# One 128x128 weight load for two heads, and slot tests as signs on ACT, in an adjacency attention with experts

## The chip, the cores and the metric

The kernel runs on one core of a Trainium2 chip. The metric is the device time of one execution in microseconds (us): the median of the timed executions.

A core has five engines that run side by side and wait for each other by semaphores. In the profile they are PE (matrix products; PEld is its loading of weights), DVE (vector), ACT (scalar, activations), POOL (GpSimd, here mostly gathers by index) and SP (it issues transfers). A product on PE has a stationary operand, the weights, which is loaded into the array, and a moving operand, whose columns stream past it. `nc.tensor.matmul(out, weights, moving)` is written in that order; the result lands in PSUM, the accumulators' memory, and ACT or DVE fetch it from there.

## The reference, cut to what matters

A layer has two parts: attention among the neighbours in a graph, then a mixture of experts with two of eight chosen for each row.

```python
# x (4096, 512), adj (4096, 4096) of zeros and ones; 8 heads of 64
h = layernorm(x)
q, k, v = (einsum('nd,hdk->hnk', h, W) for W in (Wqs, Wks, Wvs))
scores = einsum('hqk,hmk->hqm', q, k) * 64 ** -0.5
scores = scores + 0.01 * eye - 1e16 * (1 - maximum(adj, eye))
att = softmax(scores, axis=-1)
x = x + einsum('hqm,hmk,hko->qo', att, v, Wo)
# x = x + experts(layernorm(x)): routing by top 2, two layers per expert with gelu
```

The first nodes have many neighbours and the last few; all have few out of 4096.

## The kernel before: the parts that the change touches

The program has three stages.

**Stage one** projects queries, keys and values for all rows and writes them to device memory. Beside that it reads the adjacency and makes, for each tile `i` of 128 queries, a list of the keys that any of its queries has as a neighbour, so that attention skips the rest. A list is filled in chunks of 128 places. The keys are sorted by whether only the first 64 queries, only the last 64, or both need them, so that the first and last chunks of a list serve 64 queries alone (a "half" chunk). The lengths are fixed ahead:

```python
LISTED = [28, 20, 18, 16, ...]        # chunks of each of the 32 tiles; 363 in all
FIRST_ALONE = [10, 6, 5, 5, ...]      # chunks before this one: first 64 queries alone
SECOND_FROM = [25, 14, 12, 10, ...]   # chunks from this one on: last 64 queries alone

def half_of(i, c):                    # c < 0 is the tile's own 128 keys, for all queries
    if c < 0: return None
    a, b = halves[i]
    return 0 if c < a else 1 if c >= b else None
```

To turn counts into places, stage one asks of every slot of a list whether each row's run has begun, by comparing slot numbers with the run's first place. The answers (0 or 1) are weights of a product that picks the row's data by differences of neighbouring rows:

```python
def ranges(i):
    a, b = halves[i]
    return [(0, b), (a, b), (a, listed[i])]

def begun(i):
    for k, (t0, t1) in enumerate(ranges(i)):
        ...
        nc.gpsimd.tensor_scalar(          # on POOL
            started[i, k], slots[:, t0 * P : t1 * P], base[g][:, k, j : j + 1], None,
            op0=ALU.is_ge)

def list_rows(i, k):                      # one chunk t of a list
    of = [(0, 0)] if h == 0 else [(2, 3)] if h == 1 else [(0, 0), (1, 1), (2, 2)]
    for n, (q, r) in enumerate(of):
        nc.tensor.matmul(pr[:, t, :], started[i, q][:, s], row_x[g][:, r, j, :], ...)
```

POOL also gathers mask rows ahead (`pm`), which are packed into device memory, and DVE finds which keys have a flag (`neighbours`, one reduction of a 128x4096 tile for each of the 32 tiles).

**Stage two**, attention, goes through 395 items: for each tile its own keys (c = -1) and then its listed chunks. An item's keys and values come by a gather. In step n PE turns the keys of item n+3, makes the scores of item n+2 and uses the values of item n. P is 128, KD 64, NP 4 (pairs of heads), QH 64.

```python
def turn(n):                              # keys: [key, head x 64] to [head x 64, key]
    pk = ps_k.tile([P, 2, TB], F32, ...)
    for p in range(NP):
        for r in range(2):
            half = slice(r * KD, (r + 1) * KD)
            nc.tensor.transpose(pk[:, r, ts(p, KD)], kv[n][half, ts(p, P)], ident[half, half])
    nc.scalar.copy(kT[n].rearrange(...), pk[...])

def scores(n):
    s = [ps_s.tile([P, NP, P], F32, ...) for r in range(2)]
    for p in range(NP):
        for r in range(2):
            rows = slice(r * KD, (r + 1) * KD)          # one head: 64 rows of the array
            nc.tensor.matmul(part(s[r], i, c)[:, p, :], k[rows, p, :], q_in[i][rows, p, q], ...)
    for r in range(2):
        nc.scalar.activation(e[:, r * NP : (r + 1) * NP], part(s[r], i, c), AF.Exp)

def values(n):
    for p in range(NP):
        for r in range(2):
            h = 2 * p + r                               # one head: 64 columns of the array
            nc.tensor.matmul(
                po[i][r * KD : (r + 1) * KD, p, q], v[:, ts(h, KD)], e[:, r * NP + p, :], ...)
    if c >= 0:
        nc.vector.tensor_add(acc[i][:, :, q], acc[i][:, :, q], e)
```

`masked(n)` (DVE) multiplies e by the mask. At the end of a tile the sums of e (`sums`), their inverses (`rb`, a product with 128x128 weights and 128 moving columns), the output product (`py`, 128x128 weights and 512 moving columns) and the routing's transposes (`pt_b`, 128x128) follow, spread over the next items.

**Stage three** runs the experts over sorted blocks of 128 rows.

Of the kernel before, what the change touches and what calls it, by code (L numbers as in the profile page):

```python
# [43 lines left out]
def kernel(  # L44
# [174 lines left out]
    def load_q(i):  # L219
        q_in[i] = qp.tile([P, NP, P], F32, tag="q", name=f"q_{i}")  # L220
        nc.sync.dma_start(out=q_in[i], in_=qT_d[:, :, ts(i, P)])
# [46 lines left out]
    with tc.tile_pool(name="wqkv", bufs=1) as wp, tc.tile_pool(name="p1", bufs=3) as work, tc.tile_pool(  # L268
# [39 lines left out]
        )  # L308

# [21 lines left out]
        def list_constants():  # L331
# [4 lines left out]
            nc.vector.memset(again_c[:, :, :, 0:1], 0.0)  # L336
            nc.vector.tensor_scalar_mul(corner, corner, -1.0)
# [62 lines left out]
        def count_3(g):  # L400
# [24 lines left out]
            base[g] = b  # L425

        def steps(g):

# [3 lines left out]
            nc.tensor.matmul(  # L432
                pd[:, 1:], corner, x_g[:, :2], start=False, stop=True, skip_group_check=True
            )
            pe = ps_l.tile([P, G, NX], F32, tag="l", name=f"pe_{g}")
            nc.tensor.matmul(pe, step, x_g[:, 2], start=True, stop=True)
            dx = lp.tile([P, 4, G, NX], BF16, tag="dx", name=f"dx_{g}")
            nc.scalar.copy(dx[:, :3], pd)
            nc.scalar.copy(dx[:, 3], pe)
# [7 lines left out]
        def begun(i):  # L447

            g, j = divmod(i, G)
            for k, (t0, t1) in enumerate(ranges(i)):  # L450
                if t0 == t1:
# [5 lines left out]
                nc.gpsimd.tensor_scalar(  # L457
                    started[i, k], slots[:, t0 * P : t1 * P], base[g][:, k, j : j + 1], None,
                    op0=ALU.is_ge,
# [5 lines left out]
        def list_rows(i, k):  # L465
# [4 lines left out]
            for t in range(m):  # L470
                h = half_of(i, t0 + t)

                of = [(0, 0)] if h == 0 else [(2, 3)] if h == 1 else [(0, 0), (1, 1), (2, 2)]
# [8 lines left out]
        def list_keys(i, k):  # L482
# [21 lines left out]
            for h, u0, u1 in ((0, 0, a), (None, a, b), (1, b, listed[i])):  # L504
                u0, u1 = max(u0, t0), min(u1, t0 + m)
                if u0 < u1:
                    u = slice(at[i] + u0, at[i] + u1)
                    k = key[:, u0 - t0 : u1 - t0]
                    if h is None:
                        nc.vector.tensor_scalar_add(mask_of[:, u], k, float(i * (N + 1)))  # L510
                    else:
                        nc.vector.tensor_scalar(
# [102 lines left out]
        def pack():  # L615
            i, c = ready.pop(0)
            m = work.tile([P, P], F32, tag="mask", bufs=6, name=f"pm_{i}_{c}")
# [6 lines left out]
        for u in range(8 * NTB + 1):  # L624
# [26 lines left out]
            if u - 2 in load_at:  # L651
                neighbours(load_at[u - 2])
                if load_at[u - 2] == NT - 1:
# [4 lines left out]
                    q_cm = tc.tile_pool(name="q", bufs=2, side="right")  # L658
                    qp = q_cm.__enter__()
                    load_q(0)  # L660
# [41 lines left out]
    def route_1(m, l, pool, name):  # L702
# [4 lines left out]
        ahead = pool.tile([P, m, E, E], F32, tag="ahead", name=f"ahead_{name}")  # L707
        nc.vector.tensor_tensor(ahead, other, own, op=ALU.is_gt)
        same = pool.tile([P, m, E, E], F32, tag="same", name=f"same_{name}")
# [133 lines left out]
    with tc.tile_pool(name="p2a", bufs=2) as two, tc.tile_pool(  # L843
# [38 lines left out]
        def load_x(i):  # L882
            x_in[i] = two.tile([P, D], F32, tag="xt", name=f"xr_{i}")
            nc.sync.dma_start(out=x_in[i], in_=x[ts(i, P), :])
# [3 lines left out]

# [16 lines left out]
        def part(t, i, c):  # L905

            if half_of(i, c) is None:
                return t
# [195 lines left out]
        for n, (i, c) in enumerate(items):  # L1104
# [5 lines left out]
            if c == 2:  # L1110
                load_x(i)
# [307 lines left out]
```

## Time and profile before

| what | us |
|---|---|
| timed executions, median of 3 (range) | 2416.37 (2408.73 to 2416.6) |
| the profiled execution, span | 2203.7 |
| stage one, to about | 505 |
| attention, to about | 1610 |
| slot tests on POOL (L457), 96 instructions | 229.0 |
| key transposes on PE (L893), busy | 172.4 |
| scores on PE (L922), busy | 409.4 |
| values on PE (L954), busy | 311.3 |

The profiled execution was 212 us shorter than the timed ones. The busy time of a group of overlapping instructions is the time in which at least one of them ran. The ends of products on PE are modelled; their starts are the better measure, so the distance from start to start says what a group costs. A "granted clock" of 1 is the full TensorE clock.

### The profile page before, as it was taken

How to read it: one execution, taken by the hardware profiler on the slowest of the kernel's cores; microseconds unless marked ns; L12 is line 12 of the kernel's file. 1: busy time of each engine (PE TensorE's matmuls, PEld its weight loads, DVE VectorE, ACT ScalarE, POOL GpSimd, SP SyncE). 2: the span in 40 equal slices, each digit the busy share in tenths (PEclk: the TensorE clock that was granted, in tenths of full speed). 3: DMA queues.
4: the chain of work that ended last, by engine and by line, in shares of the span. 5: the costliest groups of instructions: out<-in, count | busy, mean ns of one | idle time of the engine just before them, and what ended most of it. 6: DMA issues, size and time to landing. Idle time of an engine off the chain costs nothing. (4 is left out here: it accounts for less than half of the span.)

```text
span 2203.7 us, 52479 instructions
## 1 busy us (share of the span) xinstructions
PE 2040.5 (93%) x20620; PEld 1366.7 (62%) x20620; DVE 1319.2 (60%) x2387; ACT 870.1 (39%) x1842; POOL 1242.8 (56%) x1072
## 2 busy tenths in 40 slices
PE   7877879899999999999999999999829999999998
PEld 3333334348888888888788878777614444444444
DVE  4888586724887767777677777777723222333232
ACT  2121211124666646655556555656412222222222
POOL 1769888885888657678676766667412112111112
PEclk9988988896999989999999999999959999999999
DMA  7737787847788868878788878878475556555554
GB/s 281 301 127 234 258 294 261 263 120 236 247 260 273 273 216 275 281 239 282 247 268 266 267 249 248 264 234 252 165 257 127 134 131 136 136 134 140 137 136 96
DMA packets 215039, 481.71 MB, mean 219 GB/s; under 512 B 49618, under 2 KB 81874, under 8 KB 210692
## 3 DMA queue, kind: packets, MB, share of 16 engines
q0 software_dynamic: 79232, 242.18, 37.1%
q1 hardware_dynamic: 134404, 234.01, 33.7%
q8 instruction: 168, 2.75, 0.5%
q10 hardware_dynamic: 1152, 2.10, 0.3%
q14 instruction: 83, 0.68, 0.1%
HBM read 400.59 MB, written 77.58 MB: 217 GB/s over the span
## 5 line engine op out<-in xcount | busy, mean ns | idle before, releaser
L225 POOL DMA_INDIRECT kv<-kv_d,key_of x363 | 430.4, 1186 | 231.8 <-PE po L954 136.4
L941 DVE TENSOR_TENSOR e<-e,mask 128x512 f32<-128x512 f32 (+1 forms) x363 | 322.6, 889 | 204.0 <-ACT e L932 200.4
L922 PE MATMUL s<-q,kT 64*128 64x64 f32 (+1 forms) x5808 | 409.4, 282 | 2.7 <-ACT acc L932 2.7
L1354 POOL DMA_INDIRECT out_dram<-y,r x71 | 110.6, 1558 | 474.0 <-ACT h L1324 124.7
L922 PEld LDWEIGHTS s<-q,kT 64*128 64x128 f32 x5808 | 373.4, 196 | 2.9 <-ACT acc L932 2.9
L896 ACT COPY kT<-pk 128x512 f32<-128x512 f32 x395 | 232.1, 588 | 285.1 <-PE pk L893 277.3
L932 ACT ACTIVATE e<-s 128x256 f32<-128x256 f32 (+1 forms) x726 | 297.1, 461 | 101.5 <-PE s L922 98.6
L960 DVE TENSOR_TENSOR acc<-acc,e 128x512 f32<-128x512 f32 (+1 forms) x363 | 320.4, 883 | 1.4 <-PE po L954 1.4
L954 PE MATMUL po<-e,kv 128*64 128x64 f32 (+1 forms) x5808 | 311.3, 251 | 0.0
L225 POOL DMA_INDIRECT mask<-in_adjT_dram,mask_of x230 | 257.7, 1121 | 71.9 <-issue 50.0
L457 POOL TENSOR_SCALAR started<-slots,base 128x384 bf16<-128x384 int16 (+12 forms) x96 | 229.0, 2401 | 76.6 <-DVE longer L407 75.7
L954 PEld LDWEIGHTS po<-e,kv 128*64 128x64 f32 x5808 | 246.4, 141 | 34.7 <-issue 0.8
L1318 PE MATMUL ph<-w,xT 128*128 x568 | 258.3, 598 | 0.7 <-ACT xT L207 0.7
L1347 PE MATMUL py<-w,hT 128*128 x568 | 255.6, 593 | 0.9 <-DVE hT L1332 0.9
L352 DVE TENSOR_REDUCE flags<-adjT 128x64 f32<-128x4096 f32 x32 | 141.2, 4413 | 81.2 <-DMA adjT<-in_adjT_dram 81.2
L1352 DVE TENSOR_TENSOR y<-py,bb 128x512 f32<-128x512 f32 x71 | 49.1, 692 | 225.6 <-PE py L1347 184.2
L893 PE MATMUL pk<-ident,kv 64*128 64x64 f32 x2904 | 172.4, 240 | 11.4 <-ACT kT L896 11.0
L893 PEld LDWEIGHTS pk<-ident,kv 64*128 64x128 f32 x2904 | 122.0, 142 | 77.0 <-issue 47.2
L1318 PEld LDWEIGHTS ph<-w,xT 128*128 128x128 f32 x568 | 103.2, 192 | 104.1 <-issue 103.0
L1347 PEld LDWEIGHTS py<-w,hT 128*128 128x128 f32 x568 | 102.5, 190 | 104.0 <-issue 102.8
L225 POOL DMA_INDIRECT pm<-in_adjT_dram,mask_of x133 | 130.5, 981 | 41.5 <-issue 33.6
L1353 ACT ACTIVATE y<-y,gate 128x512 f32<-128x512 f32 x71 | 51.2, 722 | 213.1 <-DVE y L1352 213.1
(589 smaller groups left out, 2405.3 us busy)
## 6 DMA issues: line engine op xcount, KB each, us to landing
adjT<-in_adjT_dram SPq DMA_DIRECT2D x32, 2048.0 KB
bb<-in_L_ffn_b_dram SPq DMA_DIRECT2D x142, 256.0 KB
r<-xs_d SPq DMA_DIRECT2D x71, 258.0 KB
kv_d<-kv SPq DMA_DIRECT2D x32, 512.0 KB
xt<-in_x_dram SPq DMA_DIRECT2D x32, 256.0 KB
qT_d<-qT SPq DMA_DIRECT2D x8, 1024.0 KB
q<-qT_d SPq DMA_DIRECT2D x32, 256.0 KB
xr<-in_x_dram SPq DMA_DIRECT2D x32, 256.0 KB
```

The source lines that it names most:

```text
L225: nc.gpsimd.indirect_dma_start(out=to, out_offset=None, in_=src, in_offset=bass.IndirectOffsetOnAxis(ap=of[:, at[i] + c : at[i] + c + 1], ...
L352: nc.vector.tensor_reduce(flags[g][:, :, j, :], adj_in.pop(i).rearrange("p c (h q) -> p h c q", h=2), axis=AX.X, op=ALU.max,)
L457: nc.gpsimd.tensor_scalar(started[i, k], slots[:, t0 * P : t1 * P], base[g][:, k, j : j + 1], None, op0=ALU.is_ge,)
L893: nc.tensor.transpose(pk[:, r, ts(p, KD)], kv[n][half, ts(p, P)], ident[half, half])
L896: nc.scalar.copy(kT[n].rearrange("k p (r j) -> k r p j", r=2), pk[:, :, : NP * KD].rearrange("k r (p j) -> k r p j", p=NP),)
L922: nc.tensor.matmul(part(s[r], i, c)[:, p, :], k[rows, p, :], q_in[i][rows, p, q], start=True, stop=True,)
L932: nc.scalar.activation(e[:, r * NP : (r + 1) * NP], part(s[r], i, c), AF.Exp)
L941: nc.vector.tensor_mul(e, e, m.unsqueeze(1).to_broadcast(e.shape))
L954: nc.tensor.matmul(po[i][r * KD : (r + 1) * KD, p, q], v[:, ts(h, KD)], e[:, r * NP + p, :], start=(c < 0 and p == 0), stop=(c == listed[i ...
L960: nc.vector.tensor_add(acc[i][:, :, q], acc[i][:, :, q], e)
L1318: nc.tensor.matmul(ph, xTs[b][:, c, :], w1[:, bass.ds(es[b], 1), c, :], start=(c == 0), stop=(c == DC - 1),)
L1347: nc.tensor.matmul(py, hTs[b][:, c, :], w2[:, bass.ds(es[b], 1), c, :], start=(c == 0), stop=(c == HC - 1),)
```

## The change

**In attention**, the two heads of a pair share one weight load of 128x128. The queries of a pair are laid out block-diagonally (each head's rows in its own half of the columns, zeros elsewhere; the zeros are written once into two fixed tiles), so that one product of 128 rows gives the scores of both heads side by side. For the values, both heads' columns of v are loaded together and both heads' e move past; of the result, the two diagonal blocks are used and the others are not. The aim is half as many products and weight loads. Keys are turned by full 128x128 transposes. The result of a tile takes two PSUM banks, and four copies on ACT (`take`) pick out the used blocks.

**In stage one**, the tests of slots move from POOL to ACT as signs (-1 or 1 in place of 0 or 1). The differences are halved, and a constant is added through one more product so that the sums come out the same. The row numbers of mask rows (`mask_of`) are written by POOL in place of DVE. Some buffers shrink to make room (`ahead`, `same`, `pm`, `xr`, `o`), and x of a tile is loaded later.

The core of the diff; cuts are marked by `...`:

```diff
 def load_q(i):
-    q_in[i] = qp.tile([P, NP, P], F32, tag="q", name=f"q_{i}")
-    nc.sync.dma_start(out=q_in[i], in_=qT_d[:, :, ts(i, P)])
+    q_in[i] = q_two[i % 2]
+    for r in range(2):
+        rows = slice(r * KD, (r + 1) * KD)
+        nc.sync.dma_start(out=q_in[i][rows, :, r, :], in_=qT_d[rows, :, ts(i, P)])
...
+            past_b = lp.tile([P, 3, G], F32, tag="past_b", name=f"past_b_{g}")
+            nc.vector.tensor_scalar(past_b, b, -1.0, 0.5, op0=ALU.mult, op1=ALU.add)
...
-            dx = lp.tile([P, 4, G, NX], BF16, tag="dx", name=f"dx_{g}")
-            nc.scalar.copy(dx[:, :3], pd)
-            nc.scalar.copy(dx[:, 3], pe)
+            dx = lp.tile([P, 5, G, NX], BF16, tag="dx", name=f"dx_{g}")
+            nc.scalar.mul(dx[:, :3], pd, 0.5)
+            nc.scalar.mul(dx[:, 3:], pe, 0.5)
...
-                nc.gpsimd.tensor_scalar(
-                    started[i, k], slots[:, t0 * P : t1 * P], base[g][:, k, j : j + 1], None,
-                    op0=ALU.is_ge,
+                nc.scalar.activation(
+                    started[i, k], slots[:, t0 * P : t1 * P], AF.Sign,
+                    bias=base[g][:, k, j : j + 1],
                 )
...
-                        nc.vector.tensor_scalar_add(mask_of[:, u], k, float(i * (N + 1)))
+                        nc.gpsimd.tensor_scalar_add(mask_of[:, u], k, float(i * (N + 1)))
...
         def turn(n):
-            for p in range(NP):
-                for r in range(2):
-                    ...
+            for p in range(NP):
+                nc.tensor.transpose(pk[:, p, :], kv[n][:, ts(p, P)], ident)
+            nc.scalar.copy(kT[n], pk)
...
         def scores(n):
-                for r in range(2):
-                    rows = slice(r * KD, (r + 1) * KD)
-                    nc.tensor.matmul(
-                        part(s[r], i, c)[:, p, :], k[rows, p, :], q_in[i][rows, p, q], ...)
+                nc.tensor.matmul(
+                    s[-1][:, p - (len(s) - 1) * NP // 2], k[:, p, :], q_in[i][:, p, :, q], ...)
...
         def values(n):
-                for r in range(2):
-                    h = 2 * p + r
-                    nc.tensor.matmul(
-                        po[i][r * KD : (r + 1) * KD, p, q], v[:, ts(h, KD)], e[:, r * NP + p, :], ...)
+                j, t = divmod(p, NP // 2)
+                nc.tensor.matmul(
+                    po[i][j][:, t, :, q], v[:, ts(p, P)], e[:, 2 * p : 2 * p + 2, :], ...)
...
+        def take(i):
+            osb[i] = single.tile([P, NP, P], F32, tag="o", name=f"o_{i}")
+            for j, t in enumerate(po.pop(i)):
+                for r in range(2):
+                    rows = slice(r * KD, (r + 1) * KD)
+                    nc.scalar.copy(osb[i][rows, ts(j, NP // 2), :], t[rows, :, r, :])
```

A half chunk (64 queries) needs one PSUM bank for the scores of all heads, a full one two.

## The prediction, made before the result was known

> **What bounds the kernel now.** I read the page's busy line first, then the busy time by stretch, then the TensorE timeline of the attention stage instruction by instruction, and last the waits of the first stage.
>
> ```profile
> PE 2040.5 (93%) x20620; PEld 1366.7 (62%) x20620; DVE 1319.2 (60%) x2387; ACT 870.1 (39%) x1842; POOL 1242.8 (56%) x1072
> ```
>
> ```profile
> 0.00:530.00 530.00, 437.19 (x1919) 220.58 (x1919) 344.04 (x693) 113.73 (x203) 391.16 (x368) 0.89 0.70 239
> 530.00:1610.00 1080.00, 1049.52 (x17001) 873.68 (x16999) 800.77 (x1311) 624.20 (x1424) 739.07 (x632) 0.97 0.80 253
> 1610.00:2204.00 594.00, 553.82 (x1705) 272.48 (x1704) 174.42 (x385) 132.15 (x215) 112.59 (x73) 0.97 0.59 137
> ```
>
> The columns are PE, PEld, DVE, ACT, POOL, then the granted clock and the DMA. The program has three stages: projections and lists (to about 505), attention (to about 1610), experts. In attention PE is busy 1049.5 of 1080 us, so a PE microsecond there is a microsecond of the end. In the first stage PE has 93 us of holes at a clock of 0.89, and POOL is the next fullest. The change leaves the third stage alone.
>
> How attention spends PE time is in the timeline of PE. Its columns are start and length in us, then line, operation, weights (rows*columns), moving tile and the count of records.
>
> ```profile
> 1019.16 0.46 PE L893 MATMUL pk<-ident,kv 64*128 64x64 f32 x8
> 1019.45 1.06 PE L922 MATMUL s<-q,kT 64*128 64x64 f32 x16
> 1020.44 0.69 PE L954 MATMUL po<-e,kv 128*64 128x64 f32 x16
> 1021.06 0.46 PE L893 MATMUL pk<-ident,kv 64*128 64x64 f32 x8
> 1021.35 1.11 PE L922 MATMUL s<-q,kT 64*128 64x128 f32 x16
> 1022.39 0.69 PE L954 MATMUL po<-e,kv 128*64 128x64 f32 x16
> 1023.01 1.16 PE L992 MATMUL rb<-rinv,spread 128*128 128x128 f32 x8
> 1024.10 0.46 PE L893 MATMUL pk<-ident,kv 64*128 64x64 f32 x8
> ...
> 1027.39 1.09 PE L954 MATMUL po<-e,kv 128*64 128x128 f32 x16
> 1028.41 3.70 PE L1001 MATMUL py<-wo,o 128*128 128x512 f32 x8
> 1032.05 0.46 PE L893 MATMUL pk<-ident,kv 64*128 64x64 f32 x8
> ```
>
> Three things are to be seen. A product of 32-bit numbers leaves two records, a transpose one. The groups follow each other without a hole. And the small products run **two at a time**: 16 score records of 128 moving columns take 1.11 us, while eight records of the same 128 columns at 128x128 (rb) take 1.16 us. The two row halves of the array work side by side for scores and transposes, and the two column halves for values. Start to start, an item costs: transposes 0.29; scores 0.99 (64 queries) or 1.04 (128); values 0.62 or 1.02. Scores hardly notice the number of queries, so they run at the pace of their weight loads; values do notice it.
>
> Two narrower windows give the pace of products that use the whole array:
>
> ```profile
> 1023.33 0.61 PE L992 MATMUL rb<-rinv,spread 128*128 128x128 f32 x4
> ```
>
> ```profile
> 1028.95 2.31 PE L1001 MATMUL py<-wo,o 128*128 128x512 f32 x5
> ```
>
> The records last 275 and 592 ns (medians of these lines), so the steps are (610-275)/3 = 112 ns at 128 columns and (2310-592)/4 = 430 ns at 512. Between them, 256 columns should step by 112 + 318/3 = 218 ns (an estimate).
>
> **What the Trainium skill says.** (1) "TensorE: Matmul & The Clock Gate", Part 3, packing small matmuls: matmuls in different row or column groups of the array run concurrently. The 16 records in 1.11 us against eight in 1.16 agree. (2) The same page, LDWEIGHTS: a load's time follows its columns, not its rows; it estimates 128 columns at 107 ns. Scores step by (1.06-0.27)/7 = 0.113 us a pair (a record lasts 0.27), nearly the same for 64 and 128 queries, which agrees. (3) "TensorEngine Tiling (Array Packing)", Key Properties: changing the tiling mode drains TensorE. rb occupies 1.09 us from its start to the next group's where eight steps of 112 ns are 0.90, so about 0.2 us goes to entering and leaving; that fits. (4) "ScalarE: Activation LUTs", What ACT_TABLE_LOAD costs: an ACTIVATE with a pointer bias takes about 280 ns + 0.833 ns an element. No instruction here has exactly this form; an estimate below uses it.
>
> **The change in attention.** The weights become 128x128. For scores, the queries of a pair of heads lie in a block diagonal with zeros, and twice the columns move; for values, both heads' columns of v meet both heads' e, and half of what is written is never read. The loads are halved, but the work side by side is lost: each pair that moved 64 or 128 columns once, on both halves of the array together, now moves 128 or 256 columns.
>
> - Transposes: 4 records of 128 columns at 0.112 = 0.45 us, from 0.29.
> - Scores, values, 64 queries: 8 x 0.112 = 0.90 each, from 0.99 and 0.62.
> - Scores, values, 128 queries: 8 x 0.218 = 1.74 each, from 1.04 and 1.02.
>
> So a half item goes from 1.90 to 2.25 us (+0.35), a full one from 2.35 to 3.93 (+1.58). The lists hold 363 items; the full ones are the sum of SECOND_FROM minus FIRST_ALONE, 134, plus the 32 own tiles, so 166 full and 229 half. 229 x 0.35 + 166 x 1.58 = 80 + 262 = **+342 us**. Against it, rb, py and the transposes of routing no longer change the mode: four such groups a tile at up to 0.2 us, 32 tiles, about -20. The four copies that take po now (one before) run on ACT while PE turns and scores, so I give them little. PE can't pass this on: it is at 97% already. DVE (800.8 us of 1080), ACT and POOL only get more room. Net in attention: **+320 us**.
>
> **The change in the first stage.** POOL loses the 96 tests:
>
> ```profile
> L457 POOL TENSOR_SCALAR started<-slots,base 128x384 bf16<-128x384 int16 (+12 forms) x96 | 229.0, 2401 | 76.6 <-DVE longer L407 75.7
> ```
>
> ```profile
> PEld L476 <- POOL started L457: 40.7, 23, 4.6
> PE pr L476 <- POOL started L457: 31.9, 20, 3.2
> ```
>
> From the page's groups and the waits (us in total, times, longest): 229 of POOL's 391 us go away. ACT gets them: 80,768 elements in each partition (128 times the sum of the ranges' lengths) x 0.833 ns + 96 x 0.28 = 94 us (estimate), on an engine busy 114 of 530. PE's two rows name the load and the product of one wait, so they aren't added: about 40 us of PE holes. Beyond them, DVE sits in the same stretch up to 2.86 us in an L510 that takes 0.16 when POOL isn't testing, POOL's mask gathers queue behind tests of 6 us, and the loads of the next adjacency tile wait behind those. All that loosens. What stays: PE's own work, about 24 records of 512 columns a tile x 32 x 0.43 = 330 us plus transposes and lists, some 390; and the transfers, 239 GB/s x 530 us = 127 MB, which at 285 GB/s (the first 60 us) need 445. The stage lasts about 505 us, so at most 60 to 100 can come back. The mask rows moved to POOL are some 100 tiny instructions and cost nothing there. I take **-55 us**.
>
> **Sum.** 2204 + 320 - 55 = about 2470 us in a profile like this one. The timed runs before are 2416, 212 us above the profiled execution, for which the profile has no reason. It does show PE at half pace at the start of attention:
>
> ```profile
> 514.82 1.91 PE L922 MATMUL s<-q,kT 64*128 64x64 f32 x16
> 516.66 1.12 PE L954 MATMUL po<-e,kv 128*64 128x64 f32 x16
> ```
>
> The same 16 records take 1.06 and 0.69 us later. If the timed runs have more of such a clock, the added PE work stretches by the same tenth (265 to 290); if full tiles ease the clock, it shrinks. I choose the plain sum, 2416 + 265 = **2680 us**.
>
> **Rivals.** (a) *Loads are the bound, and halving them pays.* For it: scores take the same time at 64 and 128 queries. If that held for all 40 loads of an item (now 20), about 0.9 us an item or 350 us would be won: 2070. Against it: rb, with one full load a record, steps by 112 ns, twice the 56 of a score record; and values follow the moving columns (0.62 to 1.02). (b) *The clock.* If the 212 us are throttled time that packed tiles cause and full ones (half zeros in the queries) don't, all could come back: 2416 + 265 - 212 = 2470. For it: 40 us at half pace in a full stretch. Against it: the rest of attention, equally packed, stands at 0.97 and more. (c) *The first stage gives everything*, 100 us and a better clock at its end: 2630. (d) *New waits*: ACT, now with signs ahead of its PSUM copies and four copies to empty po, holds up PE. Some us a tile: 2730.
>
> **Range and chances.** The attention term is firm within about 50 us, since its paces come from this trace; the first stage within 50; the unexplained 212 us of the timed runs is the widest. Range 2560 to 2770. Even (b) ends above 2% slower; only (a) makes it faster. Faster 0.04, same 0.05, slower 0.91.
>
> **What would show it.** In the profile after: score and value products with weights 128*128, eight records each, stepping about 112 ns at 128 moving columns and 218 at 256, one at a time; a full item near 3.9 us and a half one near 2.25; PE still full in attention, longer by 300 or more; DVE and POOL shares down there. In the first stage: no POOL tests, ACT up by about 95 us, no PE waits on POOL, the first attention item some 55 us earlier. I would be wrong if 256 columns step at much under 200 ns, or if the clock differs widely between the two.

## The result, and the profile after

| | us |
|---|---|
| kernel before, median (range) | 2416.48 (2408.73 to 2420.38) |
| changed kernel, median of 4 (range) | 2494.18 (2492.32 to 2498.93) |
| ratio, with its 95% interval | 1.033 (1.030 to 1.036) |

The change costs 78 us where 265 were predicted. The busy line of the page of the changed kernel (span 2490.6 us) answers to the first line shown of before:

```profile
PE 2327.0 (93%) x12728; PEld 1663.2 (67%) x12728; DVE 1274.0 (51%) x2297; ACT 982.7 (39%) x1805; POOL 1021.0 (41%) x1080
```

PE has 12,728 instructions in place of 20,620, and yet is busy 287 us longer than in the profile of before. By stretch, in the columns PE, PEld, DVE, ACT, POOL, granted clock and DMA:

```profile
0.00:530.00 530.00, 443.88 (x1926) 232.70 (x1927) 305.70 (x619) 211.36 (x314) 199.17 (x388) 0.94 0.74 248
480.00:1900.00 1420.00, 1374.92 (x9399) 1199.79 (x9397) 821.09 (x1350) 661.54 (x1316) 736.90 (x644) 0.99 0.66 197
```

In stage one POOL falls from 391 to 199 us and ACT rises from 114 to 211. In attention PE is still full, at a clock of 0.99. The timeline of PE in attention, changed kernel (start, length, line, weights, moving tile, count of records):

```profile
1018.07 1.06 PE L1022 MATMUL rb<-rinv,spread 128*128 128x128 f32 x8
1018.97 0.60 PE L915 MATMUL pk<-ident,kv 128*128 128x128 f32 x4
1019.40 1.89 PE L935 MATMUL s<-q,kT 128*128 128x256 f32 x8
1021.13 1.05 PE L976 MATMUL po<-e,kv 128*128 128x128 f32 x8
...
1024.37 1.89 PE L976 MATMUL po<-e,kv 128*128 128x256 f32 x8
1026.09 3.60 PE L1031 MATMUL py<-wo,o 128*128 128x512 f32 x8
1029.53 0.60 PE L915 MATMUL pk<-ident,kv 128*128 128x128 f32 x4
```

From start to start, turns take 0.43, scores at 128 queries 1.73 (256 moving columns), values at 128 queries as much (1026.09 - 1024.37), and values at 64 queries (128 columns) 0.89, up to the next group, at 1022.02, which is cut here. A full item comes to 0.43 + 1.73 + 1.73 = 3.89 us, where 3.93 was predicted. So the products cost what they were said to cost, and the time that is missing from the loss has to be looked for in the kernel before.

### The profile page after: what moved, and what is told of

It is laid out like the page before. It is cut to its first block, busy times and chain, and to the rows that moved or that the text cites. A ratio compares the mean times of both kernels' runs of the same rounds, so it can differ in the third digit from the quotient of the medians.

```text
span 2490.6 us, 36652 instructions
## 1 busy us (share of the span) xinstructions
PE 2327.0 (93%) x12728; PEld 1663.2 (67%) x12728; DVE 1274.0 (51%) x2297; ACT 982.7 (39%) x1805; POOL 1021.0 (41%) x1080
## 3 DMA queue, kind: packets, MB, share of 16 engines
q8 instruction: 106, 1.74, 0.3%
## 5 line engine op out<-in xcount | busy, mean ns | idle before, releaser
L228 POOL DMA_INDIRECT kv<-kv_d,key_of x363 | 446.2, 1229 | 551.3 <-PE po L976 376.5
L935 PE MATMUL s<-q,kT 128*128 128x128 f32 (+1 forms) x2904 | 499.6, 315 | 3.8 <-ACT acc L949 3.8
L976 PE MATMUL po<-e,kv 128*128 128x128 f32 (+1 forms) x2904 | 496.5, 314 | 0.7 <-issue 0.7
L976 PEld LDWEIGHTS po<-e,kv 128*128 128x128 f32 x2904 | 430.0, 192 | 30.7 <-issue 1.3
L935 PEld LDWEIGHTS s<-q,kT 128*128 128x128 f32 x2904 | 418.9, 192 | 25.4 <-ACT acc L949 4.1
L949 ACT ACTIVATE e<-s 128x512 f32<-128x512 f32 x497 | 296.3, 599 | 151.1 <-PE s L935 91.7
L228 POOL DMA_INDIRECT mask<-in_adjT_dram,mask_of x230 | 234.0, 1018 | 73.9 <-issue 68.0
L915 PE MATMUL pk<-ident,kv 128*128 128x128 f32 x1452 | 224.4, 277 | 17.7 <-ACT kT L916 11.0
L915 PEld LDWEIGHTS pk<-ident,kv 128*128 128x128 f32 x1452 | 170.6, 142 | 57.3 <-issue 36.1
L207 ACT COPY xT<-pt_e 128x512 f32<-128x512 f32 x71 | 41.5, 585 | 233.3 <-PE pt_e L206 233.3
```

The lines of the kernel that those rows point to most:

```text
L228: nc.gpsimd.indirect_dma_start(out=to, out_offset=None, in_=src, in_offset=bass.IndirectOffsetOnAxis(ap=of[:, at[i] + c : at[i] + c + 1], ...
L915: nc.tensor.transpose(pk[:, p, :], kv[n][:, ts(p, P)], ident)
L935: nc.tensor.matmul(s[-1][:, p - (len(s) - 1) * NP // 2], k[:, p, :], q_in[i][:, p, :, q], start=True, stop=True,)
L949: nc.scalar.activation(e[:, j * m : (j + 1) * m], t.rearrange("p a r q -> p (a r) q"), AF.Exp)
L976: nc.tensor.matmul(po[i][j][:, t, :, q], v[:, ts(p, P)], e[:, 2 * p : 2 * p + 2, :], start=(c < 0 and t == 0), stop=(c == listed[i] - 1), ...
```

## The experiments

Eighteen runs, told by the question. "Before" is always the kernel before on the same chip, timed beside the run; its level differs by chip, so ratios are compared. A **hole** below is an idle stretch of PE over 0.1 us after which comes a product that has no semaphore to wait for, counted between the first scores and the experts. **Half clock** is time in which the trace's clock records give TensorE half its clock; counted are the stretches that lie wholly between the first scores and the last. Those that reach over either end are told of apart. Several texts speak of the "supply theory": PE loses time because it does not get its instructions fast enough where many of them fall into a short time.

### The kernel before, seen again

Nothing is edited.

> The kernel before, unchanged, to see what its usual execution of about 2416 us looks like beside the profile of 2204 us. Clock theory: the extra 212 us are TensorE at a lower granted clock in the attention stage, where products share the array two at a time; then the executions near 2416 us have a mean granted clock of about 0.85 to 0.88, the first stage (to 505 us) and the expert stage (594 us) are as long as in the profile of 2204 us, and attention lasts about 1290 us in place of 1080. Rival, transfers or gathers are slower in the usual execution: the clock stays at 0.95, PE shows waits on DMA or POOL in attention, or all three stages stretch. Rival, a fixed cost outside the profiled span: span and time differ by 200 us.

Measured: 2429.76 us, ratio 1.001 (0.999 to 1.004), and a span of 2427.5, not 2203.7. Attention is where the two executions of the same kernel part. From the first scores to the first transpose of the experts, in this execution and then in the profile that the prediction was read from:

```profile
508.80:1854.90 1346.10, 1218.96 (x17281) 1006.53 (x17280) 823.02 (x1370) 631.62 (x1449) 732.00 (x646) 0.89 0.67 213
```

```profile
501.60:1639.40 1137.80, 1075.24 (x17282) 897.62 (x17280) 819.57 (x1370) 634.41 (x1448) 755.96 (x649) 0.95 0.79 253
```

That is 208 us more, at a clock of 0.89 against 0.95. (The 0.97 of the prediction is of 530 to 1610 and leaves out most of the half clock at both ends.) PE's timeline in this execution:

```profile
588.16 0.92 PE L954 MATMUL po<-e,kv 128*64 128x128 f32 x11
589.38 0.49 PE L954 MATMUL po<-e,kv 128*64 128x128 f32 x5 [0.30 <-issue]
...
592.90 0.38 PE L922 MATMUL s<-q,kT 64*128 64x64 f32 x2
593.91 0.77 PE L922 MATMUL s<-q,kT 64*128 64x64 f32 x9 [0.62 <-issue]
594.91 0.45 PE L922 MATMUL s<-q,kT 64*128 64x64 f32 x4 [0.23 <-issue]
```

Groups of 16 records are broken into pieces with holes between them, and "issue" says that no semaphore was waited for. Right after this, from 597.7, records last 0.42 us where they last 0.27: the clock has been halved. The view of PE's waits between 510 and 1580 us of this execution adds such idle time up (us in total, times, longest; two of its rows):

```profile
PE s L922 <- issue: 13.6, 34, 1.1
PE pk L893 <- issue: 10.9, 28, 1.1
```

The changed kernel has two rows of that kind in the same stretch:

```profile
PE pk L915 <- issue: 4.7, 7, 1.4
PE po L976 <- issue: 2.6, 5, 0.9
```

By the two windows, PE is idle 127 us of the 1346 here (1346.1 - 1219.0), 65 more than the 63 of the first profile (1137.8 - 1075.2). The rest of the 208 us lies in steps that begin at half clock: set against the median step between the same two groups in the first profile, the steps from start to start at full clock come to the same total in both executions (within 1 us), those at half clock to 144 us more. Half clock is 225 us in 28 stretches here, against 44 in 4. Of the 28, 21 begin within 7 us after a hole; the other seven follow 1.4 to 5.1 us of idle time ahead of products that had a semaphore to wait for.

### The two parts alone

The lists alone (the part of the change in stage one; attention as before):

> The stage-one part of the change alone (signs on ACT, mask rows on POOL), attention as before, packed. My step of the first stage: it ends about 55 us earlier, so about 2360 us against 2416, if the clock in attention is as low as in the usual execution before. Clock theory: mean granted clock again about 0.86. If stage one of the change were worth only the 25 to 30 us by which the first attention item starts earlier in the two profiles so far: about 2390. If the stage-one part is what makes the clock high (POOL no longer interferes): about 2180.

Measured: 2379.87 against 2428.48 us, ratio 0.979 (0.975 to 0.983), so 49 us won. The first scores start at 467.2 in place of 508.8.

Attention alone (stage one as before):

> The attention part of the change alone (128x128 weights for two heads), stage one as before. My step of attention: +320 us on the profile of 2204, so a span of about 2520, and the time like the span, because full tiles keep the clock. Clock theory: mean granted clock 0.95 to 0.97, time 2520, ratio to before about 1.043. If the clock in attention did not depend on the packing, the time would be 2416 + 320 = 2736.

Measured: 2561.89 against 2428.48, ratio 1.056 (1.051 to 1.061), so 133 us lost, clock 0.962 against 0.916. That is nearer to the 2520 of a clock that depends on the tiles than to the 2736 of one that does not. The two parts add up: 133 - 49 = 84, and the whole change costs 78. The first scores start at 535.8, 27 us later than before: part of what the attention change costs lies ahead of attention. In the first 480 us of this trace PE waits 60.5 us for the slot tests on POOL, against 32.1 in the kernel before seen again.

The lists with the mask rows left on DVE:

```diff
-                        nc.gpsimd.tensor_scalar_add(mask_of[:, u], k, float(i * (N + 1)))
+                        nc.vector.tensor_scalar_add(mask_of[:, u], k, float(i * (N + 1)))
```

> The signs on ACT alone; the mask rows stay on DVE, attention as before. My prediction gave the mask rows nothing: then 2380 us as with both. If POOL's mask rows hold back its gathers (its profile shows POOL waiting 140 us for DVE's keys in stage one): 10 to 20 us faster than both, about 2365. If DVE's relief was what helped: slower, about 2395.

Measured: 2347.31 against 2399.85, ratio 0.979 (0.975 to 0.983), the same as the lists with them. The signs on ACT do all of it, the mask rows nothing that can be measured.

### Fewer instructions in half items

The lists, and the scores of half items (64 queries) by one 128x128 load; the rest packed in pairs as before:

```diff
+            if full:
                 for p in range(NP):
                     for r in range(2):
                         nc.tensor.matmul(s[r][:, p, :], k[rows, p, :], q_in[i][rows, p, r, :], ...)
+            else:
+                for p in range(NP):
+                    nc.tensor.matmul(s[0][:, p], k[:, p, :], q_in[i][:, p, :, q], ...)
```

> Stage one of the change; in attention only the scores of half items (64 queries) go by one 128x128 load for two heads, 8 records in place of 16; full items, transposes and values stay packed. Supply theory (PE doesn't get its instructions fast enough where items are short: 80 instructions, products and loads, in 1.9 us, against 80 in 2.36 us of a full item): a half item now has 64 instructions in about the same 1.9 us, 33 in a us, as many as a full item, so the holes inside groups and the half-clock stretches at the ends of tiles go away, about 200 us: from the 2380 us of the lists alone to about 2180. Rival (packed tiles cost the clock by themselves): values and full items are packed as before, so about 2380.

Measured: 2338.99 against 2399.85, ratio 0.975 (0.971 to 0.979): hardly more than the lists alone, and near the rival's 2380 (0.98 of the 2428 that it starts from). Yet the clock changed. Beside the run with the signs alone, on the same chip, which differs from this one by the half items' scores (and by where the mask rows are written, worth nothing), the holes stay (74 of 27.1 us, for 90 of 29.1), and half clock falls from 198 us in 28 stretches to 82 in 17. The first 50 us of attention show it best, signs alone and then with half scores:

```profile
451.50:501.50 50.00, 49.54 (x626) 45.14 (x624) 25.29 (x35) 23.04 (x49) 24.13 (x22) 0.62 0.53 163
```

```profile
488.00:538.00 50.00, 46.98 (x727) 40.87 (x726) 34.76 (x39) 29.29 (x53) 34.42 (x26) 0.99 0.63 190
```

PE is busy nearly all the time in both, and the clock is 0.62 in the one and 0.99 in the other. All 20 traces agree. In the seven with packed scores in half items, the stretch of half clock that lies at the first scores is 20 to 55 us long (41.0 in the profile of before, 47.8 in the kernel before seen again); in the 13 with 128x128 scores there it is 3 to 10. So a stretch of half clock lasts longer where the scores of half items are packed. The number of instructions alone does not do it: with the 64 tiny products told of below it is 6.8 us on both chips. What in the packed scores does was not tried.

The same with all transposes at 128x128:

```diff
-                for r in range(2):
-                    nc.tensor.transpose(pk[:, r, ts(p, KD)], kv[n][half, ts(p, P)], ident[half, half])
+                nc.tensor.transpose(pk[:, p, :], kv[n][:, ts(p, P)], ident)
```

> As the run with half scores, and keys turned by four 128x128 transposes in place of eight of half size. A half item has 56 instructions, 27 in a us. Supply theory: no holes at all; the transposes cost 0.15 us more an item, 395 items, less a mode change saved: about 40 us more than the run with half scores, so 2220; if half scores alone leaves some starvation, the two are closer. Rival (packed tiles cost the clock): 2380 + 40.

Measured: 2331.33 against 2399.85, ratio 0.971 (0.967 to 0.974); 48 holes, 41 us of half clock. Both missed the supply theory's number by 100 us or more: I had taken the holes to go at once. They stand where instructions are still dense: 31 of the 48 lie ahead of or inside the packed values of half items, whose 16 products and 16 loads take 0.62 us, 52 a us.

The changed kernel with only the full items packed again (scores and values; all turns at 128x128):

> The changed kernel with full items packed again: half items (64 queries) take their scores and values by one 128x128 load for two heads (40 instructions in 2.25 us, 18 in a us), full items by two tiles at a time as before (72 in about 2.5 us). Supply theory: no holes, half items at 2.25 us where they now take about 3.2 at the ends of tiles, so attention about 110 us shorter than with the lists alone: about 2250 to 2280, the fastest so far. If instead what a packed kernel loses is tied to packed tiles: full items still lose clock, about 2350. If my cost of a half item were all that counts (2.25 against 1.9): 2380 + 80 = 2460.

Measured: 2352.44 against 2412.57, ratio 0.976 (0.973 to 0.980), the number of the rival by which packed full items lose clock. But that is not what happened: the holes are nearly gone (10, and 17 us of half clock), with the full items packed. It is not quicker for another reason. The timeline of PE shows it, in full items of this kernel:

```profile
599.80 0.66 PE L915 MATMUL pk<-ident,kv 128*128 128x128 f32 x4
600.39 1.16 PE L933 MATMUL s<-q,kT 64*128 64x128 f32 x16
601.48 1.09 PE L982 MATMUL po<-e,kv 128*64 128x128 f32 x16
602.50 0.66 PE L915 MATMUL pk<-ident,kv 128*128 128x128 f32 x4
```

A full item takes 602.50 - 599.80 = 2.70 us and not the 2.35 that it took with packed turns: the turns take 0.59 for 0.29, of which 0.14 is the full array (0.43) and the rest comes where the tiling changes to that of the packed scores. 166 x 0.35 is 58 us, most of the miss. So the last of these kernels packs everything of full items, turns too, and half items have scores and turns at 128x128:

```diff
+            if half_of(*items[n]) is not None:
+                for p in range(NP):
+                    nc.tensor.transpose(pk[:, 0, ts(p, P)], kv[n][:, ts(p, P)], ident)
+                nc.scalar.copy(kT[n], pk[:, 0, :].rearrange("k (p j) -> k p j", p=NP))
+                return
```

> The half-scores kernel (lists part of the change, scores of half items by one 128x128 load, everything of full items packed), with the transposes of half items at 128x128 as well and those of the 166 full items left packed in pairs. The supply theory: a half item gives PE 56 instructions instead of 80 in about the same 1.9 to 2.0 us, so the holes are at most those of the kernel with half scores and all turns at 128x128 (ratio 0.9705, half clock 34 us), and 166 full items save 0.2 to 0.3 us of transposes each against it, 33 to 50 us: about 0.953 of before, some 2290 us. The rival, that the packed transposes of full items bring mode changes and holes that cost as much as they save: 0.970 to 0.976, no better than the two kernels it comes from.

Measured: 2222.09 against **2212.12** us, ratio 1.005 (1.003 to 1.007). Neither number was expected, because the kernel before itself took 2212 us on this chip, in all of 12 executions (2203.5 to 2217.3). The trace of this run has not one hole. A half item takes 2.10 us in it (turns 0.49, scores 0.99, values 0.62, from start to start), 0.20 more than before; 229 x 0.20 = 46 us, about what the lists win, and nothing else is given back. On another chip, where before took 2407.73, the same kernel was run again:

> The kernel with the scores and transposes of half items at 128x128 and everything of full items packed, on another chip. Where before takes about 2212: again 1.005. Where it takes 2400 to 2430: the supply theory gives 2290 (0.953), half clock 35 us or less; the rival, that packed transposes of full items bring holes and mode changes of their own, gives 0.970 to 0.976.

Measured: 2336.13, ratio 0.971 (0.967 to 0.974), with 42 holes and 51 us of half clock: the rival's number. Packing the turns of full items again gained nothing over turning everything at 128x128. Of its holes 23 again lie at the packed values of half items.

### Work added to the kernel before

If PE loses time because it gets its instructions too slowly there, work that needs few instructions should cost less than it takes. The kernel before, with zero products added to the accumulators of 197 half items, one of 256 columns:

```diff
+            if half_of(i, c) is not None and c < listed[i] - 1:
+                nc.tensor.matmul(po[i][:, :2, :], zeros, v[:, : 2 * P], start=False, stop=False, ...)
```

> The kernel before, with work added: in 197 half items one more product of zero weights 128x128 and 256 moving columns, added into the values' accumulator (it adds zeros, so the output stays). 4 more instructions in about 0.64 us (two records of 0.218 and a mode change of 0.2): 126 us of PE in all. Supply theory: 84 instructions in 2.55 us are 33 in a us, so the supply keeps up and most of the about 220 us lost at the tile ends comes back: 2429 + 126 - 200 = about 2350, faster with more work. Rivals (packing or the clock by itself, or waits on other engines): 2429 + 126 = 2555 or more.

Measured: 2435.06 against 2399.85, ratio 1.017 (1.013 to 1.021): 35 us for 126 us of work, in between the two expectations; half clock fell to 92 us. Two of 512 columns each:

```diff
+                for _ in range(2):
+                    nc.tensor.matmul(po[i][:, :, :], zeros, v, start=False, stop=False, ...)
```

> The kernel before with more filler: two products of zero weights and 512 moving columns in each of 197 half items, 8 instructions in about 1.92 us (4 records of 0.43 and a mode change of 0.2), 378 us of PE in all; packing untouched. A half item then has 88 instructions in 3.8 us, 23 in a us, fewer than in the run with half scores and 128x128 turns. Supply theory: the bursts of holes (0.75 us apart, some ten instructions in each, nothing waited for) and the half-clock time (about 210 us of attention) nearly vanish, so the quick execution's 2204 us plus 378: about 2580 to 2620. If packed tiles lose the clock by themselves: before plus 378, 2780 to 2810, and the half-clock time stays.

Measured: 2607.55 against 2412.57, ratio 1.081 (1.077 to 1.085): 195 us for 378 us of work, clock 0.964, half clock 38 us, 28 holes (80 in the kernel before seen again). **183 us came back**, the supply theory's number, with all packing as it was. On a second chip:

> The kernel before with two zero products of 512 columns in 197 half items, 378 us of PE work, on another chip. Where before takes about 2212 us there are no holes to absorb them: about 2590 us, the full 378, ratio 1.17. Where it takes 2400 to 2430: again about 2607, ratio 1.08.

Measured: 2595.56 against 2407.73, ratio 1.077 (1.073 to 1.081), 188 us for 378. The 378 themselves were never seen, since the run did not fall on the chip where before takes 2212.

### Small instructions added to the changed kernel

The opposite edit tells the rate of instructions from the packed tiles: the changed kernel, all at 128x128, gets many products with one moving column of zeros in 197 half items, 32 in the first run:

```diff
+                for u in range(32):
+                    nc.tensor.matmul(po[i][u % 2][:, 0, 0, :1], zeros, ones[:, :1], start=False, stop=False, ...)
```

> The changed kernel, all full 128x128 tiles, with 32 tiny products (zero bf16 weights, one moving column, added into the accumulator) in each of 197 half items: 104 instructions in an item in place of 40. No packing anywhere in it. Supply theory: bursts of holes inside groups appear and half-clock time rises from 20 us to 50 or more; time 2494 + 197 x 32 x 0.03 to 0.06 us (190 to 380) plus what the holes cost. If packing is what costs the clock: no holes, clock stays at 0.97, and 2690 to 2870 by the tiny products alone.

Measured: 2694.81 against 2412.57, ratio 1.118 (1.114 to 1.122), 46 holes, but only 34 us of half clock. Undecided: the holes came, the half clock and the time did not. Then 64:

> The changed kernel with 64 tiny 16-bit products (one moving column of zeros) added in each of 197 half items, where 32 were before. A half item then gives PE 168 instructions in about 2.23 + 64 x 0.025 = 3.83 us, 44 a us, as many as the half items of the kernel before (42). Without any loss the 64 cost 197 x 1.6 = 315 us over the changed kernel: about 2800 us. If the rate of instructions alone makes the holes and the half clock, both come back: over 80 holes without a wait in attention, over 100 us of half clock, 2900 us or more. If they belong to the packed tiles, holes stay near those with 32 tiny products (46) and the half clock under 40 us: 2800 to 2850 us.

Measured: 2787.93 against 2212.12, ratio 1.264 (1.260 to 1.267), no hole, half clock 10 us. It fell on the chip where the kernel before takes 2212 us, so it decides nothing alone. On the chip where before takes 2407.73:

> The changed kernel with 64 tiny products in 197 half items, 44 instructions a us there, on another chip. Where before takes about 2212: again 2788. Where it takes 2400 to 2430: if the rate of instructions alone makes the holes, over 80 holes without a wait in attention, over 100 us of half clock and 2900 us or more; if they belong to the packed tiles, fewer than 50 holes, under 40 us of half clock and 2800 to 2850 us.

Measured: **3066.85** us, ratio 1.275 (1.270 to 1.280), 248 holes of 105 us and 338 us of half clock. The same program differs by 279 us between the two chips. The whole stretch of attention, in the first line on the chip where before takes 2212:

```profile
500.00:2200.00 1700.00, 1666.90 (x21769) 1500.62 (x21765) 824.49 (x1344) 664.15 (x1304) 740.22 (x638) 0.99 0.54 165
```

and on the chip where it takes 2408:

```profile
500.00:2490.00 1990.00, 1845.83 (x21878) 1641.52 (x21877) 826.82 (x1347) 664.79 (x1307) 739.88 (x639) 0.91 0.46 142
```

The group of 64 in PE's timeline, on the first chip:

```profile
1118.66 1.74 PE L985 MATMUL po<-ones,zeros 128*128 128x1 bf16 x64
1120.26 0.63 PE L703 MATMUL pt_b<-ident,rows 128*128 128x128 f32 x4
```

and on the second:

```profile
1104.59 1.22 PE L985 MATMUL po<-ones,zeros 128*128 128x1 bf16 x41
1106.33 0.27 PE L985 MATMUL po<-ones,zeros 128*128 128x1 bf16 x5 [0.52 <-issue]
1107.06 0.27 PE L985 MATMUL po<-ones,zeros 128*128 128x1 bf16 x5 [0.46 <-issue]
1107.79 0.28 PE L985 MATMUL po<-ones,zeros 128*128 128x1 bf16 x5 [0.46 <-issue]
1108.54 0.35 PE L985 MATMUL po<-ones,zeros 128*128 128x1 bf16 x8 [0.48 <-issue]
```

On the first, 64 products take 1.60 us, 25 ns each. On the second, 41 go at that pace, and then PE gets five products, with their five weight loads, every 0.73 us, with half a microsecond of nothing between. The next turns run at half clock (1108.76 to 1109.64, 0.88 us from start to start for 0.43). No tile here is packed, so **such holes need no packing: a large number of instructions in a short time is enough for them**, on one chip and not on the other. The 338 us of half clock come in 63 stretches, 61 of which begin within 7 us after a hole, but they are short (5.4 us in the mean, 8.0 in the kernel before).

### The changed kernel on the two kinds of chip

> The changed kernel, unaltered, on another chip. If the 212 us belong to the chip: where the kernel before takes about 2212 us, the changed one takes 2480 to 2500, a ratio of 1.12 to 1.13; where it takes 2400 to 2430, 2490 to 2500 and 1.03. So the changed kernel's time hardly depends on the chip while that of before does. The rival, that a quick chip speeds up everything alike (2212/2416 = 0.915): 2280 us and 1.03 on both.

Measured: 2485.87 against 2407.73, ratio 1.032 (1.027 to 1.037).

> The changed kernel, unaltered, once more, in the hope of the other kind of chip. Where before takes about 2212 us: 2470 to 2500, a ratio of 1.12 to 1.13, if the 212 us belong to chip and instruction rate; 1.03 if a quick chip speeds up everything alike. Where before takes 2400 to 2430: 1.03 as on two chips already.

Measured: 2493.63 against 2419.30, ratio 1.032 (1.026 to 1.037).

> The changed kernel, unaltered, a last time. Where before takes about 2212 us: 2470 to 2500, ratio 1.12 to 1.13 by the theory that the 212 us belong to chip and instruction rate; 1.03 by the rival that a quick chip speeds up everything alike. Where before takes 2400 to 2430: 1.03 again.

Measured: **2461.42 against 2196.97, ratio 1.120** (1.114 to 1.126). This run came to the same chip as the 2212. The time is 9 us under the expected range, the ratio in it. The difference is 264.5 us. Its attention stretch, changed kernel on this chip:

```profile
470.00:1890.00 1420.00, 1374.17 (x9432) 1200.87 (x9430) 828.32 (x1369) 672.54 (x1321) 764.97 (x654) 0.98 0.67 203
```

Attention looks as it does on the other chips (PE 1374 of 1420 us there and here). The changed kernel hardly knows on which chip it runs (2461 to 2494); the kernel before does:

| chip, as numbered by the runs | kernel before, median us | executions |
|---|---|---|
| 1, 8, 2, 13, 0 | 2428, 2400, 2413, 2408, 2419 | 55, all within 2390 to 2443 |
| 11, on two occasions | 2212, 2197 | 19, all within 2186 to 2218 |

One chip of six is of the quick kind. Instructions of a half item (products and loads, both as records) over the time that it takes without loss, and what the traces hold, on the chips other than 11:

| kernel | instructions a us | holes (us) | half clock, us |
|---|---|---|---|
| changed kernel | 40/2.23 = 18 | 3 (1) | 20 |
| half items at 128x128, full ones packed | 18 (full items 72/2.70 = 27) | 10 (4) | 17 |
| half scores and turns at 128x128 | 56/2.10 = 27 | 48 (20) | 41 |
| changed, 32 tiny products | 104/3.03 = 34 | 46 (23) | 34 |
| before | 80/1.90 = 42 | 80 (26) | 225 |
| changed, 64 tiny products | 168/3.83 = 44 | 248 (105) | 338 |

These are means over an item; inside it the packed values ask for 52. On chip 11 neither 44 a us nor the kernel with half items' scores and turns at 128x128 has a hole, and nor has the profile of before that the prediction was read from, if it is of that kind (42).

## Why the prediction was wrong, step by step

**The paces of attention: right.** 0.90 and 1.74 for a group of eight at 128 and 256 columns were predicted, 0.89 and 1.73 measured; a half item 2.25 and a full one 3.93, against 2.21 to 2.23 and 3.89. The mode changes too: rb takes 0.90 from start to start where it took 1.09, and py 3.44 where it took 3.64, 0.2 us each as put.

**Stage one, -55: right, as a part by itself.** The lists alone gave 49, on a chip of the other kind. The signs cost ACT what was estimated (94 us): the changed kernel's group of them, by line, with its busy time and mean, reads

```profile
L475 ACT ACTIVATE started<-slots,past_b 128x384 bf16<-128x384 int16 (+12 forms) x96 | 89.0, 992 | 74.4 <-DVE within L504 27.6 <-DVE past_b L434 27.3 <-DVE hi L424 11.2
```

and PE no longer waits for POOL there. That the mask rows on POOL are worth nothing held as well.

**The sum, +265: right on one kind of chip, in part by luck.** Chip 11 gave +264.5. By the time of the first scores it divides otherwise than the prediction had it, with the profile of before as the start: -20 ahead (501.6 to 481.4) where -55 was put, and +277 after (1138 to 1415) where +320 was put. The two misses have opposite signs and cancel. Ahead, the lists alone brought the first scores 42 us forward, but attention alone moved them 27 back, which the prediction had at nothing. What in it does that (the zeros that POOL writes into the query tiles, the two loads of queries, the smaller buffers and the later load of x are candidates) was not tried. After, the first profile holds 120 us of half clock and 63 of idle PE in its attention, ends included, and the changed kernel on chip 11 holds 54 and 50. That is worth some 33 + 12 us (an estimate: half of the difference in half clock, all of that in idle time), which a sum of paces leaves out and which makes up the 43 between 277 and 320. If the lists win 49 on chip 11 too, which was not run, the attention part as a whole costs about 314 there.

**From the sum to the timed runs, "I choose the plain sum, 2416 + 265": this step failed.** It treated the 212 us by which the timed executions exceeded the profile as a part of the program that the change leaves alone, or stretches by a tenth. They were a loss of the kernel before on five of the six chips: its half items ask for 42 instructions a us, PE is left without for some tenths of a microsecond at a time (65 us more of idle PE), and it runs at half clock more often, for longer where half scores are packed (144 us more). The changed kernel asks for 18, packs neither scores nor values, and loses little: 2490 on those chips where it takes 2461 on chip 11, against 2416 and some 2205 for before. Before loses 211 us there and the changed kernel 29, so 182 came back: 265 - 182 = 83, and 78 were measured.

**The rivals.** (b), "the clock", had the number (2470) and a large part of the cause. That throttled time would come back was right. That packed tiles bring it is right in part: with the holes nearly the same, half clock fell from 198 to 82 us when the scores of half items alone were unpacked. But packing alone does not bring it: with full items packed and half ones not, half clock is 17 us, and tiny products at full tiles bring holes and half clock too. What I held against it, that "the rest of attention, equally packed, stands at 0.97 and more", was read from the one execution that did not have the loss; it could say nothing of those that had it. (a), loads as the bound, fell with the paces; (c) gave stage one 100 us, and it gave 49; (d), new waits, is not in attention: the waits of PE on ACT come to some 16 us between 510 and 1580 (kT 8.7, o 6.8), and in the first profile to 20. It is in stage one: in its first 480 us PE's waits on DVE's x rise from 19.0 to 38.3 us and those on ACT's xn from 27.5 to 33.3, while the 31.1 on POOL's tests go.

**The rival experiments set aside.** That chip 11 speeds up everything alike (a ratio of 1.03 on it as well) is refuted by 1.120.

**What stays open.** What differs between chip 11 and the other five, or their set-up, is not shown; nor why PE gets its instructions at ten in 0.73 us, nor how many it holds in store. The transfers on the instruction queue of the traces do not explain it: the kernel with 64 tiny products has 205 of 16 KB on either chip, each about 1.0 us long, and its holes begin anywhere from 0.1 to 18 us after the last of them. That the profile of before is from a chip of the kind of 11 is inferred from its time, its lack of holes and its clock (0.949; the 19 executions on chip 11 have 0.950 to 0.962). How much of the half clock in the kernel before comes from holes and how much from packed half scores was not separated.

## What to carry to other kernels

When the profiled execution and the timed ones differ by more than the scatter, find out which of the two the change will be measured against before adding a difference to either: look for the same kernel's second profile, and in it for idle time put down to "issue", groups of equal products that fall into pieces, and the clock at the ends of a stage as well as in its middle. Count instructions for each microsecond of PE's densest stretch, not only PE's busy time; a version with fewer, longer products can do more work and lose less, and the same two versions can stand 0.971 on one chip and 1.005 on another. Judge such a change on more than one chip.

## What the runs showed of the hardware that was not expected

- Where PE starved, it was served about ten instructions (five products, five loads) every 0.73 us, in the kernel with 64 tiny products; on chip 11 the same instructions went at 25 ns a product without a break. The Trainium skill, "TensorE: Matmul & The Clock Gate", Part 1, gives about 25 ns as the least step of a small matmul. The traces agree (64 in 1.60 us on chip 11), but on the other chip only for the first 41.
- Half clock follows idle time in pieces. With 64 tiny products, 61 of 63 stretches begin within 7 us after a hole, and no single idle stretch in those 7 us is over 3.2 us. It does not always follow: with 32 of them, 22 of 27 clusters of holes (less than 3.4 us apart) are followed by none within 7 us. The same page, "A second HAM failure mode: psum-queue depth-cycling", tells of short idle times between groups that make the clock swing between half and full. The traces agree as to the swing (338 us of half clock in those 63 stretches, 225 us in 28 in the kernel before). That a queue of PSUM is behind it is not to be seen here: at the holes nothing is waited for.
- Packed 64-row scores of half items go with long stretches of half clock, though PE is as busy: clock 0.62 against 0.99 in the first 50 us of attention, on the same chip.
- The loss is not in proportion to the rate: 34 instructions a us made 23 us of holes and 34 us of half clock, 44 made 105 and 338.
- The result of an edit can turn with the chip. The kernel with half items' scores and turns at 128x128 gains 3% on one chip and loses 0.5% on chip 11, where a half item takes 2.10 us in place of 1.90 and nothing is given back.
